# A decoder kernel whose retrieval weights are products of the keys' exponentials, taken beside the second cross attention

## The chip, the cores and the metric

The kernel runs on one core of a Trainium2 chip. The metric is device microseconds of one execution, from its start to its end; the time of a kernel is the median of several executions. A profiled execution also records every instruction of the engines TensorE (PE, with its weight loads as PEld), VectorE (DVE), ScalarE (ACT), GpSimd (POOL) and SyncE (SP), with the semaphores that they wait for.

## The reference

Two decoder layers run over 16 blocks `x` of 128 rows and 256 columns. Each has a self attention, a cross attention on 16 blocks `ctx` and a feed-forward part, and a layer normalisation behind each of the three. The change concerns the feed-forward part of the second layer. It is the sum of a gated MLP and of a retrieval over 512 experts:

```python
n = b * s                                             # 2048 rows
queries = (hidden_states @ W_q).reshape(2, n, 64)
routing = jnp.einsum('tnd,tdk->tnk', queries, keys)   # two lists of 64 key scores for every row
scores2, idx2 = jax.lax.top_k(routing, 8)
sx, sy = scores2[0], scores2[1]
ix, iy = idx2[0], idx2[1]
all_scores = (sx[:, :, None] + sy[:, None, :]).reshape(n, 64)
all_idx = (ix[:, :, None] * 64 + iy[:, None, :]).reshape(n, 64)
scores, pk = jax.lax.top_k(all_scores, 8)
indices = jnp.take_along_axis(all_idx, pk, axis=-1)
de, ue = down_embed[indices], up_embed[indices]       # tables of 512 rows: a larger index reads row 511
ew = jax.nn.silu(jnp.einsum('nh,nkh->nk', x, de)) * jax.nn.softmax(scores, axis=-1)
experts_states = jnp.einsum('nk,nkh->nh', ew, ue)
mlp = jax.nn.silu(x @ gate_w) * (x @ up_w) @ down_w
return mlp + experts_states
```

So a row has, in each of two lists, its 8 best of 64 key scores; of the 64 sums of those it takes the 8 best, and a softmax over them gives the weights. An index is 64 times the first key's index plus the second's, and all indices from 511 on read the last expert.

## The kernel before

**Layout.** All numbers are f32. `x_t[b]` is block b, 128 rows on the partitions, 256 columns. The retrieval reads the 2048 x 128 queries as two lists of 2048 x 64, so output row 2*(R*128+p)+hf takes list one from row p of block R and list two from row p of block 8+R, columns 64*hf to 64*hf+63 of the query in both. The kernel therefore works in NR = 8 groups R, each with two halves `hf` of 128 rows. The weights of one group are a tile `E` of 128 x 2 x 512: a full row of 512 experts for every row, with zeros where an expert isn't chosen. That way no table is gathered: two dense matrix products with all 512 experts do the work.

**The two attentions of the second layer** are laid out in beats by `by_beats`. A block of the cross attention has 4 units of scores, one per beat. Each unit is a product into a PSUM tile `ps_st` of 128 x 1024, whose row maximum DVE takes (`nm`); six beats later the scores are computed a second time, with the maximum subtracted, and ACT takes their exponential `pT`. The sums over values and over ones go to `ps_o`. Beside the units stand jobs, each with an offset in beats from the first unit of its block; those of one beat are issued in the order of their list, behind the beat's units:

```python
        cross_block = (
            4, 6, cross_scores(pl, 8, kept1, 6),
            [(3, cross_parts), (4, cross_maxima), (11, cross_out), (12, cross_invert), (13, cross_add), (14, cross_scale),
             (1, values), (-2, queries), (18, turn_block), (19, route), (23, lambda b: score(0, b)),
             (25, lambda b: score(1, b)), (26, best)],
            [b for R in range(NR) for b in (R, NR + R)],
        )
```

`cross_out` copies `ps_o` to `ol` on ACT; `cross_invert` turns the sums over ones into their reciprocals by a logarithm and an exponential on ACT; `cross_add` adds the residual (`xn`) on DVE and takes the statistics of the normalisation, of which POOL computes `rstd` by a power; `cross_scale` normalises into `x_t[b]` on DVE. `queries` makes the masked copies `z` on POOL. `turn_block` transposes the finished block, and ACT copies it into `fxT`, the transposed input of the last feed-forward part. `route`, `score` and `best` run only for the second block of a group (b = 8+R): `route` multiplies with W_q (`fq_T` is the copy on ACT), `score` multiplies with the keys, once per half (ACT copies into `rt`), and `best` takes on DVE the 8 best of each list (`sv`), the 64 sums of these (`al`) and the 8 best sums (`sc`). These four hold all groups at once, in a pool `early`. The small products share one PSUM bank in two halves (`ps_half`); three tiles of two banks each serve `ps_st`.

In the beats, `vec`, `act` and `pool` issue through a wrapper at L199 that keeps the program's order, so every operation of DVE, ACT and POOL there has the line L199. TensorE's order is always kept: all products go through `mm` (L240) and all transposes through `turned` (L243). In the last block the activations that go through `act` keep the program's order (L1478); the rest is placed by a scheduler that looks at what each engine has to do.

**The last block** (from L1465 on) begins with a loop over R = 0 to 8. In each round `weights(R)` computes `E[R]` on DVE and ACT, TensorE computes three items of the gated MLP (`gate_up`: two products of 128 x 512 each into two `ps_f` banks of four, SiLU of the one to `g` on ACT, their product to `gT` on DVE), and then the eight 128 x 128 transposes of `E[R-1]` into `ps_x`, which ACT copies to `eT` (L1540). Of the 32 items 24 stand in this loop and 8 later.

`weights(R)` computes for both halves: the 512 sums `S` of the first 8 keys of list one (whole, unsorted) with all 64 of list two, which are the scores of experts 0 to 511 (DVE, L1486); `top`, the negated best sum; on ACT, per half, the exponentials `w8` of the 8 best sums with their total `z`, `wl` of the 64 best pairs and `ex` of the 512 sums, all minus the best; the mask `m` of the 64 pairs that are at least as large as the eighth best (`is_ge` with `al`), less those whose first key is one of 0 to 7, times `wl`, summed to `rest`, the weight that goes to expert 511; then per half the mask `M` of the 512 sums, its count on ACT (`none`, L1529), and E = M / z * ex (L1530), with `rest` added to the last column. The counts are summed at the end; a branch (L1640) on a total above zero would handle rows with equal scores one by one, and isn't taken here. ACT uses one table for exponentials and another for SiLU and loads one when it needs it (ACT_TABLE_LOAD). Behind the branch come `down` (product with all 512 expert rows, SiLU, times `eT`), the last 8 items, `finish` and the output.

Of the kernel before, what the change touches and what calls it, by code (L numbers as in the profile page):

```python
# [9 lines left out]
F32 = mybir.dt.float32  # L10
# [8 lines left out]
P = 128  # L19
# [12 lines left out]
def kernel(ctx: ExitStack, tc: tile.TileContext, a: dict, out: bass.AP):  # L32
# [1217 lines left out]
    sv = early.tile([P, NR, 2, 2, 8], F32, name="sv")  # L1250
    al = early.tile([P, NR, 2, 8, 8], F32, name="al")
    sc = early.tile([P, NR, 2, 8], F32, name="sc")
    with ExitStack() as st:
        pl, switch = attention_tiles(st, 6)
# [170 lines left out]
        def score(hf, b):  # L1425
            R = b - NR
            if R < 0:
                return
            ps = pl["m"].tile([P, 2, 64], F32, name="ps_m")
            rows = slice(hf * 64, hf * 64 + 64)  # L1430
            for t in range(2):
                mm(ps[:, t, :], lhsT=routes[R][rows, t, :], rhs=fkeys[rows, t, :], start=True, stop=True)
            act.copy(rt[:, R, hf], ps)

        def best(b):
            R = b - NR
            if R < 0:
                return
            for hf in range(2):
                for t in range(2):  # L1440
                    vec.max(sv[:, R, hf, t, :], rt[:, R, hf, t, :])
            vec.tensor_tensor(
                al[:, R], sv[:, R, :, 0, :].unsqueeze(3).to_broadcast([P, 2, 8, 8]),
                sv[:, R, :, 1, :].unsqueeze(2).to_broadcast([P, 2, 8, 8]), ALU.add,
            )
            for hf in range(2):
                vec.max(sc[:, R, hf, :], al[:, R, hf].rearrange("p i j -> p (i j)"))

# [3 lines left out]
             (1, values), (-2, queries), (18, turn_block), (19, route), (23, lambda b: score(0, b)),  # L1452
             (25, lambda b: score(1, b)), (26, best)],
            [b for R in range(NR) for b in (R, NR + R)],
# [7 lines left out]
    with ExitStack() as st:  # L1462
# [17 lines left out]
        def weights(R):  # L1480
# [8 lines left out]
            )  # L1489
            top = hp.tile([P, 2], F32, name="top")  # L1490
            nc.vector.tensor_scalar_mul(top, sc[:, R, :, 0], -1.0)
            w8 = hp.tile([P, 2, 8], F32, name="w8")
            wl = hp.tile([P, 2, 64], F32, name="wl")
            ex = hp.tile([P, 2, 512], F32, name="ex")
            z = hp.tile([P, 2], F32, name="z")
            for hf in range(2):
                one = top[:, hf : hf + 1]
                act(w8[:, hf, :], sc[:, R, hf, :], AF.Exp, bias=one, accum_out=z[:, hf : hf + 1])
                act(wl[:, hf, :], al[:, R, hf].rearrange("p i j -> p (i j)"), AF.Exp, bias=one)
                act(ex[:, hf, :], S[:, hf].rearrange("p a b -> p (a b)"), AF.Exp, bias=one)  # L1500
            rz = hp.tile([P, 2], F32, name="rz")
            nc.vector.reciprocal(rz, z)

            si = hp.tile([P, 2, 8], U32, name="si")
            for hf in range(2):
# [5 lines left out]
            nc.vector.tensor_tensor(  # L1511
                m, al[:, R], sc[:, R, :, 7:8].unsqueeze(3).to_broadcast([P, 2, 8, 8]), ALU.is_ge
            )
# [4 lines left out]
            nc.vector.tensor_tensor(m, m, mo, ALU.subtract)  # L1518
            nc.vector.tensor_tensor(m.rearrange("p h i j -> p h (i j)"), m.rearrange("p h i j -> p h (i j)"), wl, ALU.mult)
            rest = hp.tile([P, 2], F32, name="rest")  # L1520
# [60 lines left out]
        equal = nc.values_load(n_equal[0:1, 0:1], min_val=0, max_val=P * NR * 2 * 1024)  # L1581

        def chosen_one_by_one(st):

# [58 lines left out]

        first.close()
        hp = st.enter_context(tc.tile_pool(name="ffn_b", bufs=2))
# [115 lines left out]
```

## Time and profile before

| | us |
|---|---|
| median of 3 executions | 1466.75 (1464.52 to 1467.91) |
| profiled execution | 1463.26 |
| its span, first to last instruction | 1461.5 |
| mean granted TensorE clock | 0.954 |

Busy time by stage, in us, from the profile's busy time in windows of the span:

| window | what runs | PE | DVE | ACT | POOL | clock |
|---|---|---|---|---|---|---|
| 1186 to 1212 | end of the cross attention, first `weights` | 21.85 | 14.64 | 13.18 | 1.60 | 0.81 |
| 1212 to 1240 | first rounds of the last block | 27.49 | 18.73 | 19.42 | 0.00 | 1.00 |
| 1240 to 1300 | further rounds | 54.90 | 32.25 | 43.41 | 0.00 | 1.00 |
| 1300 to 1315 | last round, counts, branch | 12.10 | 4.51 | 7.50 | 0.00 | 0.89 |
| 1315 to 1461.5 | `down`, last items, `finish` | 135.83 | 42.06 | 14.06 | 8.80 | 0.98 |

A timeline line has the start in us, the length in us, the engine, the line of the program, the operation, what it writes and reads with partitions x elements and types, how many such instructions the line stands for, and in brackets an idle time ahead of it and what ended that. A group line has the count, the busy time and the mean in ns of one. A line of the waits has the us waited in all, the count and the longest in us. L199, L240, L243 and L1478 are lines of helpers, so the tile's name tells the operations of such a line apart.

### The profile page before, as it was taken

To read this page: it belongs to the slowest core of one execution; us is meant where nothing else is said; L and a number is where in the kernel's file an instruction comes from. 1 tells how busy PE (TensorE), PEld (TensorE's weight loads), DVE (VectorE), ACT (ScalarE), POOL (GpSimd) and SP (SyncE) were. 2 spreads that over 40 slices of the span, in tenths; PEclk is the share of its full clock that TensorE was granted. 3 is DMA by queue.
4 is the path that set the end of the run, shared out by engine and by line. 5 is a ranking of instruction groups with operands and counts; after the bars stand their busy time and mean duration, and the time that the engine had idled before them with its cause. 6 is when DMAs were issued, how large, how long until landed. Compare 5 with 4: busy or idle time off the path is not lost. (4 is left out here: it accounts for less than half of the span.)

```text
span 1461.5 us, 28762 instructions
## 1 busy us (share of the span) xinstructions
PE 1332.1 (91%) x11929; PEld 850.8 (58%) x11929; DVE 818.3 (56%) x2179; ACT 598.3 (41%) x1051; POOL 292.4 (20%) x402
## 2 busy tenths in 40 slices
PE   3999889999999945999999779999999989989997
PEld 2656555555555523777788646666555544446666
DVE  6899877787878641100001158876777756533222
ACT  1454425556556621111111125553566656761010
POOL 7000243334454120000000053311222200000000
PEclk9999979999999976999999959999999999999999
DMA  9100000000000005233222011112000000000000
GB/s 309 57 2 2 2 1 2 1 2 16 16 16 16 16 31 189 84 99 103 92 90 84 28 51 31 31 33 86 2 2 2 2 2 1 0 1 15 15 8 22
DMA packets 42716, 57.01 MB, mean 39 GB/s; under 512 B 5928, under 2 KB 32568, under 8 KB 42568
## 3 DMA queue, kind: packets, MB, share of 16 engines
q1 hardware_dynamic: 34808, 37.79, 8.1%
q0 software_dynamic: 4544, 12.21, 2.6%
q10 hardware_dynamic: 3216, 4.99, 1.0%
q8 instruction: 98, 1.61, 0.5%
q14 instruction: 50, 0.41, 0.1%
HBM read 38.60 MB, written 16.38 MB: 38 GB/s over the span
## 5 line engine op out<-in xcount | busy, mean ns | idle before, releaser
L199 DVE TENSOR_REDUCE nm<-ps_st 128x4 f32<-128x1024 f32 (+1 forms) x256 | 312.6, 1221 | 116.2 <-PE ps_st L240 115.8
L199 ACT ACTIVATE pT<-ps_st 128x1024 f32<-128x1024 f32 x224 | 229.4, 1024 | 192.0 <-PE ps_st L240 190.6
L199 POOL TENSOR_TENSOR rstd<-ve,nhalf 128x1 f32<-128x1 f32 x112 | 62.6, 561 | 683.8 <-DVE ve L199 657.1
L240 PE MATMUL ps_o<-pT,v 128*32 128x256 f32 (+1 forms) x2560 | 164.6, 348 | 1.1 <-DVE oT L199 1.1
L240 PE MATMUL ps_st<-rot,z 32*128 32x256 f32 x1024 | 150.9, 415 | 2.3 <-DVE nm L199 2.3
L1135 DVE TENSOR_TENSOR ye<-ps_e,b 128x256 f32<-128x256 f32 (+6 forms) x38 | 16.1, 424 | 236.9 <-PE ps_e L1132 236.9
L240 PE MATMUL ps_st<-z,rot 32*128 32x512 f32 x512 | 134.7, 604 | 0.0
L1124 ACT ACTIVATE h<-ps_h,b 128x672 f32<-128x672 f32 (+7 forms) x64 | 46.6, 727 | 204.3 <-PE ps_h L1120 192.3
L1120 PE MATMUL ps_h<-h,w 128*128 128x336 f32 (+7 forms) x512 | 122.1, 399 | 0.0
L1120 PEld LDWEIGHTS ps_h<-h,w 128*128 128x128 f32 x512 | 97.2, 190 | 23.6
L240 PEld LDWEIGHTS ps_o<-pT,v 128*32 128x32 f32 x2560 | 54.4, 108 | 95.9 <-issue 86.0
L240 PE MATMUL ps_st<-nmT,pick 32*128 32x256 bf16 x1024 | 101.3, 276 | 2.6 <-ACT pT L199 2.5
L240 PEld LDWEIGHTS ps_st<-rot,z 32*128 32x128 f32 x1024 | 92.9, 192 | 16.6 <-issue 4.9
L199 POOL DMA_INDIRECT y<-ys,place x32 | 31.2, 976 | 283.0 <-DVE absT L1260 275.3
L240 PE MATMUL ps_o<-pT,ones 128*32 128x256 f32 x1024 | 78.7, 379 | 0.0
L240 PEld LDWEIGHTS <-pick 32*128 32x128 bf16 x1024 | 29.2, 92 | 74.6 <-issue 67.8
L240 PE MATMUL ps_st<-ctx,z 32*128 32x256 f32 x512 | 72.2, 399 | 0.0
L240 PE MATMUL ps_f<-fxT,fgw 128*128 128x512 f32 x128 | 62.2, 609 | 6.7 <-ACT g L1478 6.7
L1132 PE MATMUL ps_e<-w,h 128*128 128x256 f32 (+6 forms) x304 | 67.3, 379 | 0.0
L1120 PE MATMUL ps_h<-xeT,w 128*128 128x336 f32 (+7 forms) x256 | 65.3, 415 | 2.1 <-DVE xeT L1112 2.1
L240 PE MATMUL ps_st<-z,ctx 32*128 32x512 f32 x256 | 65.4, 589 | 0.0
L1132 PEld LDWEIGHTS ps_e<-w,h 128*128 128x128 f32 (+6 forms) x304 | 54.9, 181 | 11.0 <-issue 1.0
(311 smaller groups left out, 2348.4 us busy)
## 6 DMA issues: line engine op xcount, KB each, us to landing
w<-in_W_dram SPq DMA_DIRECT2D x16, 512.0 KB, 3.6
w<-in_W_dram SPq DMA_DIRECT2D x8, 1024.0 KB, 6.6
xs<-zero SPq DMA_DIRECT2D x42, 128.0 KB, 3.9
xe<-xs SPq DMA_DIRECT2D x32, 128.0 KB, 3.8
ys<-ye SPq DMA_DIRECT2D x32, 128.0 KB, 2.9
x<-in_x_dram SPq DMA_DIRECT2D x16, 128.0 KB, 5.9
ctx<-in_ctx_dram POOLq DMA_DIRECT2D x16, 128.0 KB, 5.5
out_dram<-x SPq DMA_DIRECT2D x16, 128.0 KB, 1.7
```

The costliest lines, as they stand in the source:

```text
L199: instruction = getattr(self.engine, name)(*args, **kw)
L240: tc.keep_in_program_order(nc.tensor.matmul(*args, **kw))
L1120: nc.tensor.matmul(ps[:, n, 0:H], lhsT=w[:, c, hc * P : (hc + 1) * P], rhs=src[:, c, n * H : (n + 1) * H], start=(c == 0), stop=(c == part ...
L1124: nc.scalar.activation(dst[:, hc, 0:cap].rearrange("p (n t) -> p n t", n=2), ps[:, :, 0:H], AF.Gelu, bias=b12[:, layer, hc : hc + 1],)
L1132: nc.tensor.matmul(ps[0:m], lhsT=h2[:, fc, c : c + m], rhs=w3[:, fc, :], start=(fc == 0), stop=(fc == 3))
L1135: nc.vector.tensor_add(ye[0:m, c // P, :], ps[0:m], b3[0:m])
```

## The change

The exponential of a sum is the product of two exponentials. The change computes exponentials of the keys themselves, each less the best key of its list, in the cross attention of the second layer, and multiplies them in the last block.

- `best(b)` no longer keeps the 64 sums `al` for every group; it also writes `least`, the three negated maxima (of the two lists and of the sums), with two DVE operations.
- A new job `exponentials(hf, b)`, 28 and 30 beats from the first unit of the block, issues five ACT exponentials per half: `e0` of the first 8 keys of list one (8 columns), `e1` of all 64 of list two, `ev` of the 8 best of each list (twice 8 columns) and `e8` of the 8 best sums, with their total `ez`. As `route`, it does so for the second block of a group only: 16 halves in all. The results stay in `early`.
- `weights(R)` loses `top` and all its activations but the count `none`. `wl` becomes a DVE product of the two rows of `ev` (128 x 128), and `ex` a product of `e0` and `e1` on POOL (128 x 1024, one operation for both halves; both operands are read repeatedly along one dimension). The sums for the mask `m` are computed again on DVE (128 x 128). The reciprocal reads `ez`.
- The pool of `weights` is closed ahead of the branch instead of behind it.

The order of TensorE's products is the same before and after. In the order after, POOL has the two products `ex` of R = 0 and 1 ahead of the `rstd` of the last block of the cross attention, and DVE has `S`, `wl` and the first half of `E` of R = 0 ahead of that block's `x`.

```diff
--- before.py
+++ after.py
@@ -1248,8 +1248,14 @@
 
     rt = early.tile([P, NR, 2, 2, 64], F32, name="rt")
     sv = early.tile([P, NR, 2, 2, 8], F32, name="sv")
-    al = early.tile([P, NR, 2, 8, 8], F32, name="al")
     sc = early.tile([P, NR, 2, 8], F32, name="sc")
+
+
+    e0 = early.tile([P, NR, 2, 8], F32, name="e0")
+    e1 = early.tile([P, NR, 2, 64], F32, name="e1")
+    ev = early.tile([P, NR, 2, 2, 8], F32, name="ev")
+    e8 = early.tile([P, NR, 2, 8], F32, name="e8")
+    ez = early.tile([P, NR, 2], F32, name="ez")
     with ExitStack() as st:
         pl, switch = attention_tiles(st, 6)
 
@@ -1439,18 +1445,36 @@
             for hf in range(2):
                 for t in range(2):
                     vec.max(sv[:, R, hf, t, :], rt[:, R, hf, t, :])
+            al = pl["w"].tile([P, 2, 8, 8], F32, name="al")
             vec.tensor_tensor(
-                al[:, R], sv[:, R, :, 0, :].unsqueeze(3).to_broadcast([P, 2, 8, 8]),
+                al, sv[:, R, :, 0, :].unsqueeze(3).to_broadcast([P, 2, 8, 8]),
                 sv[:, R, :, 1, :].unsqueeze(2).to_broadcast([P, 2, 8, 8]), ALU.add,
             )
             for hf in range(2):
-                vec.max(sc[:, R, hf, :], al[:, R, hf].rearrange("p i j -> p (i j)"))
+                vec.max(sc[:, R, hf, :], al[:, hf].rearrange("p i j -> p (i j)"))
+            least = routes[R] = pl["w"].tile([P, 3, 2], F32, name="least")
+            vec.tensor_scalar_mul(least[:, 0:2, :].rearrange("p t h -> p h t"), sv[:, R, :, :, 0], -1.0)
+            vec.tensor_scalar_mul(least[:, 2, :], sc[:, R, :, 0], -1.0)
+
+        def exponentials(hf, b):
+            R = b - NR
+            if R < 0:
+                return
+            least = routes[R]
+            act.activation(e0[:, R, hf, :], rt[:, R, hf, 0, 0:8], AF.Exp, bias=least[:, 0, hf : hf + 1])
+            act.activation(e1[:, R, hf, :], rt[:, R, hf, 1, :], AF.Exp, bias=least[:, 1, hf : hf + 1])
+            for t in range(2):
+                act.activation(ev[:, R, hf, t, :], sv[:, R, hf, t, :], AF.Exp, bias=least[:, t, hf : hf + 1])
+            act.activation(
+                e8[:, R, hf, :], sc[:, R, hf, :], AF.Exp, bias=least[:, 2, hf : hf + 1],
+                accum_out=ez[:, R, hf : hf + 1],
+            )
 
         cross_block = (
             4, 6, cross_scores(pl, 8, kept1, 6),
             [(3, cross_parts), (4, cross_maxima), (11, cross_out), (12, cross_invert), (13, cross_add), (14, cross_scale),
              (1, values), (-2, queries), (18, turn_block), (19, route), (23, lambda b: score(0, b)),
-             (25, lambda b: score(1, b)), (26, best)],
+             (25, lambda b: score(1, b)), (26, best), (28, lambda b: exponentials(0, b)), (30, lambda b: exponentials(1, b))],
             [b for R in range(NR) for b in (R, NR + R)],
         )
         ordered[0] = True
@@ -1487,19 +1511,18 @@
                 S, rt[:, R, :, 0, 0:8].unsqueeze(3).to_broadcast(all512),
                 rt[:, R, :, 1, :].unsqueeze(2).to_broadcast(all512), ALU.add,
             )
-            top = hp.tile([P, 2], F32, name="top")
-            nc.vector.tensor_scalar_mul(top, sc[:, R, :, 0], -1.0)
-            w8 = hp.tile([P, 2, 8], F32, name="w8")
-            wl = hp.tile([P, 2, 64], F32, name="wl")
+            wl = hp.tile([P, 2, 8, 8], F32, name="wl")
+            nc.vector.tensor_tensor(
+                wl, ev[:, R, :, 0, :].unsqueeze(3).to_broadcast([P, 2, 8, 8]),
+                ev[:, R, :, 1, :].unsqueeze(2).to_broadcast([P, 2, 8, 8]), ALU.mult,
+            )
             ex = hp.tile([P, 2, 512], F32, name="ex")
-            z = hp.tile([P, 2], F32, name="z")
-            for hf in range(2):
-                one = top[:, hf : hf + 1]
-                act(w8[:, hf, :], sc[:, R, hf, :], AF.Exp, bias=one, accum_out=z[:, hf : hf + 1])
-                act(wl[:, hf, :], al[:, R, hf].rearrange("p i j -> p (i j)"), AF.Exp, bias=one)
-                act(ex[:, hf, :], S[:, hf].rearrange("p a b -> p (a b)"), AF.Exp, bias=one)
+            nc.gpsimd.tensor_tensor(
+                ex.rearrange("p h (a b) -> p h a b", a=8), e0[:, R].unsqueeze(3).to_broadcast(all512),
+                e1[:, R].unsqueeze(2).to_broadcast(all512), ALU.mult,
+            )
             rz = hp.tile([P, 2], F32, name="rz")
-            nc.vector.reciprocal(rz, z)
+            nc.vector.reciprocal(rz, ez[:, R])
 
             si = hp.tile([P, 2, 8], U32, name="si")
             for hf in range(2):
@@ -1509,14 +1532,18 @@
             nc.vector.tensor_scalar(own, own, 7.5, None, ALU.is_lt)
             m = hp.tile([P, 2, 8, 8], F32, name="m64")
             nc.vector.tensor_tensor(
-                m, al[:, R], sc[:, R, :, 7:8].unsqueeze(3).to_broadcast([P, 2, 8, 8]), ALU.is_ge
+                m, sv[:, R, :, 0, :].unsqueeze(3).to_broadcast([P, 2, 8, 8]),
+                sv[:, R, :, 1, :].unsqueeze(2).to_broadcast([P, 2, 8, 8]), ALU.add,
+            )
+            nc.vector.tensor_tensor(
+                m, m, sc[:, R, :, 7:8].unsqueeze(3).to_broadcast([P, 2, 8, 8]), ALU.is_ge
             )
             mo = hp.tile([P, 2, 8, 8], F32, name="mo")
             nc.vector.tensor_tensor(mo, m, own.unsqueeze(3).to_broadcast([P, 2, 8, 8]), ALU.mult)
             nc.vector.tensor_reduce(counts[:, R, :, 0], m.rearrange("p h i j -> p h (i j)"), AX.X, ALU.add)
             nc.vector.tensor_reduce(counts[:, R, :, 1], mo.rearrange("p h i j -> p h (i j)"), AX.X, ALU.add)
             nc.vector.tensor_tensor(m, m, mo, ALU.subtract)
-            nc.vector.tensor_tensor(m.rearrange("p h i j -> p h (i j)"), m.rearrange("p h i j -> p h (i j)"), wl, ALU.mult)
+            nc.vector.tensor_tensor(m, m, wl, ALU.mult)
             rest = hp.tile([P, 2], F32, name="rest")
             nc.vector.tensor_reduce(rest, m.rearrange("p h i j -> p h (i j)"), AX.X, ALU.add)
             E = hp.tile([P, 2, 512], F32, name="E")
@@ -1579,6 +1606,8 @@
         n_equal = sp.tile([P, 1], I32, name="n_equal")
         nc.vector.tensor_copy(n_equal, ps)
         equal = nc.values_load(n_equal[0:1, 0:1], min_val=0, max_val=P * NR * 2 * 1024)
+
+        first.close()
 
         def chosen_one_by_one(st):
 
@@ -1641,7 +1670,6 @@
             with ExitStack() as st2:
                 chosen_one_by_one(st2)
 
-        first.close()
         hp = st.enter_context(tc.tile_pool(name="ffn_b", bufs=2))
 
         def down(tb):
```

## The prediction

> **What bounds the kernel now.** I read the page first, then the waits of TensorE in the last block, then the timeline, because an average over 1461.5 us says nothing of a stage of 115 us.
>
> ```profile
> span 1461.5 us, 28762 instructions
> PE 1332.1 (91%) x11929; PEld 850.8 (58%) x11929; DVE 818.3 (56%) x2179; ACT 598.3 (41%) x1051; POOL 292.4 (20%) x402
> ```
>
> TensorE is the bound of the whole; only a place where it stands still can give time back. The wait summary of TensorE from 1196 us to the branch at 1311.2 us:
>
> ```profile
> PE ps_f L240 <- ACT g L1478: 6.7, 6, 1.1
> PE ps_half L243 <- DVE x L199: 1.5, 1, 1.5
> ```
>
> Six waits of 1.1 us on the SiLU `g`, and in the tail of the cross attention one of 1.5 us on the last block's normalised rows `x`. The timeline shows one such round:
>
> ```profile
> 1261.45 0.71 ACT L1478 ACTIVATE ex<-S,top 128x512 f32<-128x512 f32 x1
> ...
> 1263.05 0.63 ACT L1529 ACTIVATE none<-M 128x512 bf16<-128x512 bf16 x1 [0.90 <-DVE M L1525]
> ...
> 1263.79 1.28 ACT L1478 ACT_TABLE_LOAD   x1
> ...
> 1265.09 1.09 ACT L1478 ACTIVATE g<-ps_f 128x512 f32<-128x512 f32 x2
> ...
> 1265.73 1.98 PE L240 MATMUL ps_f<-fxT,fgw 128*128 128x512 f32 x4 [1.12 <-ACT g L1478]
> ...
> 1269.27 1.04 PE L243 MATMUL ps_x<-ident,E 128*128 128x128 f32 x8
> ...
> 1281.84 1.04 PE L243 MATMUL ps_x<-ident,E 128*128 128x128 f32 x8
> ```
>
> ACT does six exponentials, waits for a mask, reloads its table (1.28 us), and only then frees the PSUM bank that TensorE needs. A round lasts 1281.84 - 1269.27 = 12.57 us. What it lasts without the wait stands earlier, in the first rounds:
>
> ```profile
> 1221.28 1.88 PE L240 MATMUL ps_f<-fxT,fgw 128*128 128x512 f32 x4
> ...
> 1231.58 1.04 PE L243 MATMUL ps_x<-ident,E 128*128 128x128 f32 x8
> 1232.46 1.88 PE L240 MATMUL ps_f<-fxT,fgw 128*128 128x512 f32 x4
> ```
>
> Three items take 10.30 us and the transposes 0.88 us: 11.18 us.
>
> **The change, part by part.** The profiled execution took 1463.26 us (span 1461.5), 3.5 us under the median 1466.75 of the three runs. I sum differences against the profiled execution and put them on the median.
>
> *1. Exponentials and table loads leave the rounds.* ACT then has per round two masks (0.63 + 0.19 each), three `g` (0.60) and two `eT` (0.62): 4.7 us, no table load. Six rounds fall from 12.57 to 11.18 us: 6 x 1.39 = **-8.3 us**. What is late next? DVE is busy 32.2 us in the six slices from 1240 to 1300, so 6.8 us per round; `wl` and the rebuilt sums add 2 x 0.28 and `top` (0.16) goes: 7.2 us. If one POOL multiply stops it for its whole length (2.6 us, below) that is 9.8 of 11.18: still under TensorE. The exponentials of the last R come behind the first `g`, so one pair of table loads stays: 1.28 + 2.26 + 1.28 = 4.8 us between the first and second `g`. TensorE needs the second `g` only for its fourth item, 10.3 us after its start, and the second `g` ends near 9.3: nothing.
>
> *2. Ten small exponentials per R in the cross attention.* Rows of the same sizes: `w` (128x8) 0.30 and `wl` (128x64) 0.33 us, but they overlap: `w` and its accumulator read take 0.29 from start to start, so about 0.20 without the read; `wl` 0.24. One half (8, 64, 8, 8 columns, the last with read): 0.20 + 0.24 + 0.40 + 0.29 = 1.13 us, 16 halves. The first half of an R stands behind the pair of `ol` and ahead of a score exponential `pT`. ACT, then TensorE:
>
> ```profile
> 1116.63 0.87 ACT L199 ACTIVATE ol<-ol 128x256 f32<-128x256 f32 x2
> 1117.56 1.02 ACT L199 ACTIVATE pT<-ps_st 128x1024 f32<-128x1024 f32 x1
> ```
>
> ```profile
> 1118.83 0.48 PE L240 MATMUL ps_st<-ctx,z 32*128 32x256 f32 x2
> ```
>
> ACT has no gap there: `pT` would end near 1119.57 instead of 1118.58, and TensorE rewrites that bank at 1118.83 to 1119.15. It comes 0.4 to 0.8 us late; part returns, since the two row groups that normally share this stretch then run apart. Bounds per place 0 and 0.8; I take 0.5, the middle. Four R (0 to 3) have score tiles behind them: **+2.0 us** (0 to 3.2). The second half stands where ACT idles 0.82 us: `pT` comes 0.3 us late against a reserve of 0.8, nothing. DVE's two added `least` (0.16 each) lie ahead of a maximum whose result has about 0.5 us to spare: nothing; without that cover 8 x 0.3 = 2.4 us.
>
> *3. The tail on ACT.* The two halves of R = 6 (2.26 us) stand between `fq_T` (1206.62 to 1206.99) and the next `rt` (1208.20), where 1.2 us were idle: **+1.0 us** before TensorE reaches the first item. Those of R = 5 delay a `fkeys` product, which is over before the last `x` arrives: nothing.
>
> *4. The tail on POOL and DVE.* The sums `S` and POOL's new multiply `ex` are both released by the last `ps_o` product. POOL has two multiplies (R = 0, 1) queued ahead of the `rstd` of the last block; DVE has `wl`, a reciprocal, the rebuilt sums and one `E` (waiting for `ex`) ahead of the last `x`.
>
> ```profile
> 1197.75 1.22 DVE L1486 TENSOR_TENSOR S<-rt 128x1024 f32<-128x1024 f32 x1 [0.22 <-PE ps_o L240]
> ...
> 1202.83 0.41 DVE L199 TENSOR_SCALAR x<-xn,mv,rstd 128x256 f32<-128x256 f32 x1 [0.26 <-POOL rstd L199]
> ```
>
> ```profile
> 1202.24 0.55 POOL L199 TENSOR_TENSOR rstd<-ve,nhalf 128x1 f32<-128x1 f32 x1 [6.39 <-DVE ve L199]
> ```
>
> How long does a 128x1024 multiply take on POOL? Nearest row, one group of POOL:
>
> ```profile
> L199 POOL TENSOR_TENSOR rot<-rot,rot_t 128x256 f32<-128x256 f32 x32 | 23.2, 726 | 2.5
> ```
>
> The MEMSET rows (128x64 0.14, 128x1024 0.94 us) give 0.83 ns per column and a fixed part of 0.09. Lower bound 0.73 + 768 x 0.83 ns = 1.4 us, upper four of the slower `rot_t` rows, 3.3 us; taken 0.09 + 4 x 0.64 = 2.6 us, by the row of the same operation. Unhindered the pair ends at 1197.8 + 5.2 = 1203.0, and `rstd` starts 0.8 us late.
>
> DVE and POOL hinder each other here:
>
> ```profile
> 149.65 2.74 POOL L199 TENSOR_SCALAR z<-rot,hm 128x256 f32<-128x256 f32 x3
> ...
> 150.59 0.60 DVE L199 TENSOR_SCALAR x<-xn,mv,rstd 128x256 f32<-128x256 f32 x1
> ```
>
> This normalisation takes 0.40 us alone and 0.60 beside `z`; and `rot_t` (0.82) differs from `rot` (0.73) in that a DVE product runs when it starts. If the two exclude each other fully, about 2.1 us of each multiply stand in front of DVE (0.5 lies beside index searches), and 0.3 us of added DVE work: 2 x 2.1 + 0.3 = 4.5 us. Bounds 0.6 and 4.5; I take **+3.3 us**, nearer to the upper, because `S`, `wl`, `E` and the mask all read two tensors or a wide one from SBUF.
>
> The row first: delays of 0.2 us beside POOL operations of 0.9. [...]
>
> *5. The rest.* The pool closed ahead of the branch leaves the 1.5 us of the branch, and what follows runs in the same order on TensorE: nothing; bound one more such wait, +1.5 us.
>
> Sum: -8.3 + 2.0 + 1.0 + 3.3 = **-2.0 us**, 1464.75 us (1461.3 for an execution like the profiled one).
>
> **The rivals.**
>
> *A, the sum above*: own range -5.5 to +1.5 us (1461.25 to 1468.25), from the bounds of steps 2 and 4.
>
> *B, no exclusion*: POOL and DVE run side by side, step 4 costs 0.6: -8.3 + 2.0 + 1.0 + 0.6 = -4.7, 1462.05 us. For it: several normalisations started 0.32 us into a `z` took their usual 0.40. Against it: the 0.60 above.
>
> *C, slower: the multiply itself*. Its place is the tail, where two stand ahead of `rstd`. With full exclusion the cost is about 2X - 0.7, and above 2.6 us the first rounds, which wait for the same multiplies, stall by about twice the excess. It decides from X = 3 us; at X = 4: -8.3 + 2.0 + 1.0 + 7.3 + 2.8 = +4.8, 1471.55 us. For it: operands repeated along a dimension, which no row of POOL has. Against: the 0.73 of `rot` would have to grow more than fivefold for four times the columns.
>
> *D, slower: the cross attention*. If all ten halves of R = 0 to 4 stall TensorE for 0.8 us, step 2 costs 8 instead of 2: +4.0, 1470.75 us. Against: ACT's idle 0.82 us before every second one.
>
> **How the numbers follow.** A 0.47, B 0.25, C 0.18, D 0.10. Predicted is A. 0.2% is 2.9 us, about what a measurement of this kernel can tell from no change. Of A 0.36 lies beyond -2.9 and 0.06 beyond +2.9; of B nearly 0.9 is faster; of C and D nearly 0.9 slower. Faster 0.17 + 0.23 = 0.40; slower 0.03 + 0.24 = 0.27; within 0.33. The range, 1460.0 to 1472.0, takes in B with a cheap step 2 and C and D at their prices.
>
> **What would show it.** Step 1: no wait of TensorE on `g` in the rounds, rounds of 11.2 us, three table loads there. Step 2: TensorE waiting for `pT` about 0.5 us once per R. Step 3: `rt` 1 us later behind `fq_T`. Step 4: the length of `ex`; `S`, `M`, `xn` longer or later beside it; the wait for the last `x` grown from 1.5 to about 5 us. The prediction is wrong if TensorE still waits in the rounds (for `gT` or `E` then), or if `ex` takes over 3 us or under 1.5.

## The result and the profile after

The changed kernel takes 1460.01 us (median of 15, 1458.48 to 1464.18) against 1466.32 us for the kernel before, measured beside it (median of 15, 1462.14 to 1468.32). The ratio is 0.9967, with a 95% interval of 0.9957 to 0.9978: 4.8 us faster, 3.2 to 6.3. Two later measurements on other occasions gave 0.9988 (0.9972 to 1.0004) and 0.9991 (0.9978 to 1.0005). The forecast was -2.0 us, 1464.75 us, in a range of 1460.0 to 1472.0.

The page of the changed kernel begins with its span, then the busy time of each engine:

```profile
span 1462.5 us, 28806 instructions
PE 1333.3 (91%) x11929; PEld 853.1 (58%) x11929; DVE 837.2 (57%) x2203; ACT 580.0 (40%) x1071; POOL 311.6 (21%) x410
```

This profiled execution took 1464.18 us, the longest of its 15, while the first profile of before (1463.26 us) was one of its kernel's shorter ones. The two spans alone would say that nothing was gained. So I compared the traces place by place: TensorE's products come in the same order in both, and the difference of the start times of the same product tells how far one execution has fallen behind the other. Where that lag changes, time is lost or won. The places are the cross attention (1040 to 1190 us of before), the tail (1190 to 1237), the rounds (to 1309) and the branch (to 1325):

| against the first profile of before, us | cross attention | tail | rounds | branch | sum |
|---|---|---|---|---|---|
| changed kernel | +2.52 | +4.25 | -8.35 | -1.81 | -3.4 |
| changed_again | +2.49 | +5.61 | -8.35 | -1.85 | -2.1 |
| changed_third | +2.49 | +4.40 | -8.35 | -1.83 | -3.3 |
| before_again | 0.00 | +0.07 | +0.01 | +0.07 | +0.1 |

Ahead of 1040 us the lag is between -3.9 and +4.3 us, in code that is the same in all of them, so the whole of one execution says little; behind 1325 us it does not change by 0.01 us. The mean times of the three measurements of the changed kernel lie 4.8, 1.7 and 2.0 us below those of the kernel before.

The rounds first. The timeline of the changed kernel, all engines, one round:

```profile
1265.02 1.04 PE L243 MATMUL ps_x<-ident,E 128*128 128x128 f32 x8
...
1268.27 1.22 DVE L1510 TENSOR_TENSOR S<-rt 128x1024 f32<-128x1024 f32 x1
1268.29 0.58 ACT L1502 ACTIVATE g<-ps_f 128x512 f32<-128x512 f32 x1
1268.53 2.72 POOL L1520 TENSOR_TENSOR ex<-e,e 128x1024 f32<-128x1024 f32 x1 [8.46 <-ACT none L1556]
...
1269.41 1.86 DVE L1558 SCALAR_TENSOR_TENSOR E<-rest,rz,E 128x1 f32<-128x1 f32 x1
...
1276.19 1.04 PE L243 MATMUL ps_x<-ident,E 128*128 128x128 f32 x8
```

From transposes to transposes it is 1276.19 - 1265.02 = 11.17 us, with no table load and no wait of TensorE. DVE is held up there (an `E` of one column takes 1.86 us, 0.22 us elsewhere), and it costs nothing. The waits of TensorE from 1190 to 1318 us show where time is lost instead:

```profile
PE ps_half L243 <- DVE x L199: 3.2, 1, 3.2
PE ps_half L240 <- ACT fxT L199: 2.1, 2, 1.7
PE ps_half L240 <- ACT rt L199: 1.8, 2, 1.2
PE ps_f L240 <- PEq L1669: 1.4, 1, 1.4
```

The six waits on `g` are gone; the wait for the last `x` has grown from 1.5 to 3.2 us, and those for `fxT` and `rt` from 1.0 and 0.7 to 2.1 and 1.8. The last two stood in the kernel before, over the same window, as

```profile
PE ps_half L240 <- ACT fxT L199: 1.0, 2, 0.6
PE ps_half L240 <- ACT rt L199: 0.7, 2, 0.4
```

### The profile page after: what moved, and what is told of

Same layout as the page of the kernel before. It is cut to its first block, busy times and chain, and to the rows that moved or that the text cites. A ratio compares the mean times of both kernels' runs of the same rounds, so it can differ in the third digit from the quotient of the medians.

```text
span 1462.5 us, 28806 instructions
## 1 busy us (share of the span) xinstructions
PE 1333.3 (91%) x11929; PEld 853.1 (58%) x11929; DVE 837.2 (57%) x2203; ACT 580.0 (40%) x1071; POOL 311.6 (21%) x410
## 5 line engine op out<-in xcount | busy, mean ns | idle before, releaser
L199 ACT ACTIVATE pT<-ps_st 128x1024 f32<-128x1024 f32 x224 | 229.3, 1024 | 184.6 <-PE ps_st L240 183.7
```

Source lines behind the costliest of these rows:

```text
L199: instruction = getattr(self.engine, name)(*args, **kw)
```

## The experiments

### The added part alone, and its place on ACT

**exps_only** adds to the kernel before what the change adds in the cross attention, and leaves `weights` as it was:

```diff
+            least = routes[R] = pl["w"].tile([P, 3, 2], F32, name="least")
+            vec.tensor_scalar_mul(least[:, 0:2, :].rearrange("p t h -> p h t"), sv[:, R, :, :, 0], -1.0)
+            vec.tensor_scalar_mul(least[:, 2, :], sc[:, R, :, 0], -1.0)
...
+        def exponentials(hf, b):
...
-             (25, lambda b: score(1, b)), (26, best)],
+             (25, lambda b: score(1, b)), (26, best), (28, lambda b: exponentials(0, b)), (30, lambda b: exponentials(1, b))],
```

> The kernel before, with the 16 halves of small exponentials and the negated maxima added in the cross attention (their results are written and not read; they share two sets of buffers), and the pool closed ahead of the branch; the weights of the last block stay as before. So it is the added part of the change alone. Theory (the added half that stands behind the pair of `ol` delays one score exponential per group): in the trace TensorE falls behind the kernel before by 0.6 us at each of the groups R = 0 to 3, 2.5 us in all, then by about 1 us in the tail between `fq_T` and `rt`; the rounds of the last block stay at 12.57 us with their waits on `g`. Timed: +3.5 us, 1470 us, ratio 1.0024. Rival (ACT has room, the exponentials are free): 0 to 1 us, ratio 1.000 to 1.0007. Rival D (every half stalls TensorE): +8 us or more, ratio over 1.005.

Measured: 1466.76 us, ratio 1.0030 (1.0017 to 1.0043). The places: cross attention +2.51, tail +3.04, rounds -0.02, branch +0.03. The lag grows by 0.63 us at each of four groups and by nothing between them, as the theory has it; that the exponentials are free, and that every half stalls, are both ruled out. The tail lost three times what was expected. TensorE's waits from 1190 to 1318 us in this kernel:

```profile
PE ps_f L240 <- ACT g L1500: 7.0, 7, 1.1
PE ps_half L240 <- ACT fxT L199: 2.1, 2, 1.7
PE ps_half L240 <- ACT rt L199: 1.8, 2, 1.2
```

The exponentials of R = 5 delay the copy `fxT`, and TensorE waits 1.7 us for it instead of 0.6. In the changed kernel a later `x` hides that; here `x` is not late, and it counts. `fxT` and `rt` together move the lag by 1.09 - 0.38 + 0.86 = 1.6 us. The rest, 1.5 us, comes behind them: about 0.9 us where TensorE's clock is still at half when it is full in the kernel before (13.65 us of half clock in this tail instead of 10.24), and 0.6 us at a seventh wait on `g`.

**beats_29_30** is the changed kernel with one number changed:

```diff
-(28, lambda b: exponentials(0, b)), (30, lambda b: exponentials(1, b))
+(29, lambda b: exponentials(0, b)), (30, lambda b: exponentials(1, b))
```

> The changed kernel with the first half of the exponentials one beat later, beat 29 instead of 28: there it stands behind the copy `v` (0.37 us) ahead of an idle 0.82 us of ACT, no longer behind the pair of `ol` (0.87 us). Theory (place, not amount): the stall of 0.63 us per group goes to 0 to 0.3, so the kernel gains 1.3 to 2.5 us on the changed kernel, about 1458 us; the tail and the rounds stay as they are. Rival (the amount of work on ACT sets the delay): the stalls stay, 1460 us as the changed kernel.

Measured: 1457.68 us, ratio 0.9974 (0.9959 to 0.9989). The cross attention costs 0.01 us instead of 2.5. ACT's timeline in the changed kernel, at one of the four groups:

```profile
1098.76 0.87 ACT L199 ACTIVATE ol<-ol 128x256 f32<-128x256 f32 x2
1099.54 0.53 ACT L199 ACTIVATE e<-rt,least 128x8 f32<-128x8 f32 x2
...
1100.63 1.00 ACT L199 ACTIVATE pT<-ps_st 128x1024 f32<-128x1024 f32 x1
```

and in this one:

```profile
1097.36 1.02 ACT L199 ACTIVATE pT<-ps_st 128x1024 f32<-128x1024 f32 x1
1098.72 0.37 ACT L199 COPY v<-ps_half 128x256 f32<-128x256 f32 x1 [0.33 <-PE ps_half L243]
1098.98 0.54 ACT L199 ACTIVATE e<-rt,least 128x8 f32<-128x8 f32 x2
...
1100.09 1.00 ACT L199 ACTIVATE pT<-ps_st 128x1024 f32<-128x1024 f32 x1
```

The same 1.1 us of exponentials stands behind `ol` in the first (0.87 us, with no idle time) and behind `v` in the second, where ACT had been idle. The place sets the stall, not the amount. The tail did not stay as it was, as had been expected: in this execution it cost 5.03 us, more than in two of the three profiles of the changed kernel, and the sum of places is lower by 1.8 to 3.1 us (-5.2 against -2.1 to -3.4).

### What the rounds waited for

**no_exp_table** is the kernel before with SiLU in the place of the exponential in the six activations of `weights`. It leaves the exponential out, so its weights are other numbers, and it stands here for its time alone:

```diff
-                act(w8[:, hf, :], sc[:, R, hf, :], AF.Exp, bias=one, accum_out=z[:, hf : hf + 1])
-                act(wl[:, hf, :], al[:, R, hf].rearrange("p i j -> p (i j)"), AF.Exp, bias=one)
-                act(ex[:, hf, :], S[:, hf].rearrange("p a b -> p (a b)"), AF.Exp, bias=one)
+                act(w8[:, hf, :], sc[:, R, hf, :], AF.Silu, bias=one, accum_out=z[:, hf : hf + 1])
+                act(wl[:, hf, :], al[:, R, hf].rearrange("p i j -> p (i j)"), AF.Silu, bias=one)
+                act(ex[:, hf, :], S[:, hf].rearrange("p a b -> p (a b)"), AF.Silu, bias=one)
```

> The kernel before, with the six exponentials of each round replaced by SiLU of the same tiles and shapes (so the exponential is left out and the weights are other numbers); ACT does as much work, but needs no other table in the rounds. Theory (the two table loads of 1.28 us are what makes ACT late): with 2.6 us of loads gone and the 2.3 us of small work kept, ACT is ready in time, the six waits on `g` go, rounds last 11.2 us instead of 12.57, about -8.3 us, ratio 0.9943. Rival (it is the exponentials that keep `g` waiting): the waits stay at half, rounds near 12, -3 us or less. If the theory holds, taking the exponentials out of the rounds was not needed for the gain, only the change of tables had to go.

Measured: 1454.91 us, ratio 0.9946 (0.9924 to 0.9969). The places: cross attention 0.00, tail +1.21, rounds -8.35, the very number of the changed kernel, and branch -1.85. Its timeline, all engines:

```profile
1252.01 1.04 PE L243 MATMUL ps_x<-ident,E 128*128 128x128 f32 x8
...
1254.18 0.71 ACT L1478 ACTIVATE ex<-S,top 128x512 f32<-128x512 f32 x1
...
1255.31 0.71 ACT L1478 ACTIVATE ex<-S,top 128x512 f32<-128x512 f32 x1
...
1263.18 1.04 PE L243 MATMUL ps_x<-ident,E 128*128 128x128 f32 x8
```

Both `ex` are still there, 0.71 us each, and the round is 11.17 us, with no table load. So taking away the two table loads per round, 2.56 us, is enough to end the stall; activations of the size of the exponentials fit. That taking away the exponentials and keeping the loads would have been enough too isn't excluded: they are 2.26 us per round, and the stall was 1.39.

### POOL and DVE in the tail

Three kernels differ from the changed one in the product `ex` alone. **pool_in_order** wraps it, so that POOL keeps the program's order; **product_twice** issues it twice; **product_on_dve** gives it to DVE:

```diff
-            nc.gpsimd.tensor_tensor(
+            tc.keep_in_program_order(nc.gpsimd.tensor_tensor(
```

```diff
+            nc.gpsimd.tensor_tensor(
+                ex.rearrange("p h (a b) -> p h a b", a=8), e0[:, R].unsqueeze(3).to_broadcast(all512),
+                e1[:, R].unsqueeze(2).to_broadcast(all512), ALU.mult,
+            )
```

```diff
-            nc.gpsimd.tensor_tensor(
+            nc.vector.tensor_tensor(
```

> The changed kernel with POOL kept in the program's order: all eight products `ex` come behind the last `rstd` of the cross attention. Nothing else is edited. Theory (POOL's products of R = 0 and 1 stop DVE, and hold up `rstd`, ahead of the last `x`): TensorE's wait for the last `x` falls from 3.2 us to about 1.5 to 2, the tail gains 1.2 to 2 us, and the first rounds lose nothing, since `E` of R = 0 is needed only about 20 us later; about 1458.5 us. Rival (DVE's own added work is what delays `x`): the wait stays at 3.2 us and the time at 1460.

> The changed kernel with every product `ex` on POOL issued twice in a row (the same values once more into the same tile), so each group has 3.8 us of POOL in place of 1.9. Theory (POOL and DVE products with two operands from SBUF exclude each other for their whole length): two more products ahead of the last `rstd` delay the last `x` by 2 x 1.9 us, the wait grows from 3.2 to about 7 us; in the rounds DVE has 7.2 + 3.8 = 11.0 us of 11.2, so they hold or grow by up to 0.5 us each; +4 to +7 us on the changed kernel. Rival (no exclusion, only `rstd` queued behind POOL): also +3.8 us for the last `x`, but DVE's products keep their 0.28 us beside POOL and the rounds stay at 11.18 with room.

> The changed kernel with the product `ex` on DVE (128x1024, as `S`, which takes 1.22 us) and none on POOL. Theory (a POOL product stops DVE's two-operand work for its 1.9 us, so it takes nothing off DVE): `x` comes no later than in the changed kernel, the wait 3.2 us falls to 2.5 to 3.2; the rounds hold 11.18 us, since DVE has 7.2 + 1.2 = 8.4 us in each; 0 to -1.5 us on the changed kernel. Rival B (POOL runs beside DVE): DVE is burdened by 1.2 us more per product, the wait for `x` grows by 1 to 2 us, +1 to +2 us.

First what the changed kernel itself shows. POOL's timeline there:

```profile
1204.76 4.71 POOL L1520 TENSOR_TENSOR ex<-e,e 128x1024 f32<-128x1024 f32 x2 [2.09 <-PE ps_o L240]
1212.16 0.55 POOL L199 TENSOR_TENSOR rstd<-ve,nhalf 128x1 f32<-128x1 f32 x1 [2.69 <-DVE ve L199]
...
1224.87 1.90 POOL L1520 TENSOR_TENSOR ex<-e,e 128x1024 f32<-128x1024 f32 x1 [5.82 <-DVE E L1557]
```

and DVE's beside it:

```profile
1204.58 1.23 DVE L1510 TENSOR_TENSOR S<-rt 128x1024 f32<-128x1024 f32 x1
1205.72 1.99 DVE L1515 TENSOR_TENSOR wl<-ev 128x128 f32<-128x128 f32 x1
1207.63 0.15 DVE L1525 RECIPROCAL rz<-ez 128x2 f32<-128x2 f32 x1
...
1207.96 0.22 DVE L1529 FIND_INDEX8 si<-sv,rt 128x8 uint32<-128x64 f32 x1
1208.09 1.53 DVE L1534 TENSOR_TENSOR m<-sv 128x128 f32<-128x128 f32 x1
...
1224.90 2.95 DVE L1510 TENSOR_TENSOR S<-rt 128x1024 f32<-128x1024 f32 x1
```

A product takes POOL 1.90 us when nothing is in its way (1224.87). The pair at 1204.76 takes 4.71, since `S` is running and the first has to wait 0.9 us for its end; then `wl` (0.28 us elsewhere) stands for 1.99 us until the first is through, and `m` (0.28) for 1.53 until the second is. At 1224.87 POOL is 0.03 us ahead of `S`, and `S`, 1.22 us elsewhere, takes 2.95. The reciprocal and the index searches pass at their usual 0.15 and 0.22 us. So in these rows `ex` and an operation of DVE shut each other out for a whole instruction, whichever starts first, and only some operations of DVE are free of it. It isn't so beside every POOL operation: as the prediction noted, a normalisation that starts 0.32 to 0.35 us into a masked copy `z` (0.98 to 1.00 us there) takes its usual 0.40 us, eleven times in the kernel before. What sets `z` apart from `ex` no run here shows.

With full exclusion and its product of 2.6 us the prediction's formula for the tail gives 4.5 us, and its sum would have been -0.8; the product is 1.90 us here, and with 1.90 the same formula gives 3.1 and the sum -2.2.

**pool_in_order**: 1458.78 us, ratio 0.9976 (0.9959 to 0.9993). The wait for `x` falls from 3.2 to 1.6 us, the tail costs 3.36 us instead of 4.25 to 5.61, the rounds stay at -8.35. The theory holds, and its gain is cut short by the same exclusion. POOL in this kernel:

```profile
1205.20 0.66 POOL L199 TENSOR_TENSOR rstd<-ve,nhalf 128x1 f32<-128x1 f32 x1 [6.60 <-DVE ve L199]
1205.84 3.80 POOL L1520 TENSOR_TENSOR ex<-e,e 128x1024 f32<-128x1024 f32 x2
```

DVE in this kernel:

```profile
1205.90 1.98 DVE L199 TENSOR_SCALAR x<-xn,mv,rstd 128x256 f32<-128x256 f32 x1 [0.44 <-POOL rstd L199]
```

`rstd` sets off both: POOL starts the next product 0.06 us ahead of `x`, and `x`, 0.41 us elsewhere, takes 1.98.

**product_twice**: 1466.67 us, ratio 1.0026 (1.0009 to 1.0044), +5.0 us on the 1461.66 of the changed kernel in the same set of runs. Its waits of TensorE:

```profile
PE ps_half L243 <- DVE x L199: 6.8, 1, 6.8
PE ps_f L240 <- DVE gT L1584: 2.2, 1, 2.2
```

and two operations of DVE that stand between the four products:

```profile
1209.49 1.87 DVE L1535 CAST own<-si 128x16 f32<-128x16 uint32 x1
1211.27 2.19 DVE L1556 TENSOR_SCALAR M<-S,sc 128x512 bf16<-128x512 f32 x1
```

The wait for `x` is the 3.2 + 2 x 1.9 = 7.0 that was expected, nearly, and a stall of 2.2 us in the first rounds comes with it: rival C as the prediction had it, met only at twice the work. The places are +12.1 in the tail, with a second stretch of half clock of 3.4 us behind that stall, and still -8.35 in the rounds: two products per round fit into DVE's 11.2 us. A cast of 16 columns (0.16 us elsewhere) and a compare with one tensor (0.48) wait as well, so reading one tensor alone does not by itself set a DVE operation free.

**product_on_dve**: 1455.06 us, ratio 0.9952 (0.9933 to 0.9971). TensorE's waits:

```profile
PE ps_half L240 <- ACT fxT L199: 2.1, 2, 1.7
PE ps_half L240 <- ACT rt L199: 1.8, 2, 1.2
PE ps_f L240 <- PEq L1669: 1.4, 1, 1.4
```

None for the last `x`, which went further than the theory, and the tail costs 2.57 us. The rounds hold. On DVE the product takes 1.22 us; on POOL it took 1.90 us of POOL and as much of DVE. A part of the gain may be order: the scheduler now puts the last block's `xn` right behind the first product, and no run separates the two. The second measurement:

> The changed kernel with the product on DVE, again, beside the changed kernel on one chip. Its first profile had no wait for the last `x` any more, and 0.9952 in time. Theory (the wait for `x` of about 3 us was POOL's doing; the later wait for `fxT` of 1.1 us stays): 2 to 3 us below the changed kernel, ratio to the kernel before 0.9955 to 0.9975. Rival: as the changed kernel, within 1 us.

gave 1462.03 us, ratio 0.9978 (0.9961 to 0.9995), just outside what was expected, with the changed kernel at 1463.65 in the same set of runs. The places come again (+2.51, +2.62, -8.35, -1.85, sum -5.1; in the first +2.49, +2.57, -8.35, -1.84), so the trace is more constant than the time. By the mean times it is 1.6 us below the changed kernel in this set of runs and 5.3 in the other; by the places 1.7 to 3.0.

### Put together

> Both edits of the changed kernel together: exponentials at beats 29 and 30, and POOL in the program's order. Theory: the two gains lie in different places and add up, 1.3 to 2.5 and 1.2 to 2 us, so about 1456.5 us, 3 to 4 us below the changed kernel, ratio to the kernel before about 0.9935. Rival: no gain beyond 1 us.

**combined** (beats 29 and 30, and POOL in order): 1458.19 us, ratio 0.9982 (0.9968 to 0.9995), no better than either edit alone: a miss. Cross attention +0.01 and the wait for `x` 1.3 us, as expected; but the tail cost 4.30 us where POOL in order alone had 3.36, and the branch -0.12 instead of -1.85. TensorE's clock stood at half for 17.06 us of this tail (13.66 with POOL in order alone), which costs 0.94 us in the first items (1.06 us for a product that takes 0.59 there), and again behind the branch. These two took the gain back. Its windows (columns: window, its length, PE busy and products, PEclk, DMA share, GB/s):

```profile
1196.00:1200.00 4.00, 1.58 (x7) 0.78 0.00 0
...
1208.00:1212.00 4.00, 3.58 (x7) 0.50 0.00 0
1212.00:1216.00 4.00, 4.00 (x7) 0.59 0.00 0
```

> The product on DVE, and the exponentials placed by group: R = 0 to 4 and 7 at beats 29 and 30, R = 5 and 6 at offsets that put them behind the last `rt` of group 6 and of group 7, where ACT idles. Theory (each stall of the change has its place): no 0.63 us per group, TensorE's waits for `fxT` and `rt` in the tail back to 0.6 and 0.4 us, so 4 to 5 us below the kernel with only the product on DVE; the rounds at 11.18 us. In sum the loss of the change is gone and its gain of 8.3 us stays: 7 to 9 us below the kernel before, ratio 0.994 to 0.9955. Rival: the first `g` comes late behind 4.5 us of exponentials and takes back 2 us or more.

**placed** is product_on_dve with the exponentials of every group where ACT idles:

```diff
-(28, lambda b: exponentials(0, b)), (30, lambda b: exponentials(1, b))
+(lambda i: {11: 33, 13: 34}.get(i, 29), lambda b: exponentials(0, b)),
+             (lambda i: {11: 33, 13: 34}.get(i, 30), lambda b: exponentials(1, b))
```

Measured: 1456.72 us, ratio 0.9960 (0.9947 to 0.9972), beside the changed kernel's 0.9991 in the same set of runs. Of the kernels that compute the reference's weights it is the fastest by the places: cross attention 0.00, tail +2.19, rounds -8.35, branch -1.85, sum -8.0; by the mean times 6.8 us below the kernel before, a little short of the 7 to 9 that were expected. TensorE's waits:

```profile
PE ps_half L243 <- DVE x L199: 1.9, 1, 1.9
PE ps_half L240 <- ACT fxT L199: 1.4, 2, 0.8
PE ps_half L240 <- ACT rt L199: 0.7, 2, 0.4
```

`rt` is back at the 0.7 of before, and the first `g` behind 4.5 us of exponentials brings no wait. The wait for `fxT` came down to 0.8 us, not to the 0.6 of before. With TensorE sooner at the last `x`, that wait is back at 1.9 us.

### What is chance

> The changed kernel as it is, a second profiled execution and more times, on the chip of the other runs of this call. What the change does by itself should come again at the same places and sizes, against the kernel before: +0.63 us at each of the groups R = 0 to 3, the wait for the last `x` at 3.2 us, the rounds -8.3 us. What is chance should not: the stretch of half clock near 1031 us (+1.5 us in the first profile of the changed kernel) and the missing one behind the branch (-1.4 us). Time 4 to 6 us below the kernel before, ratio 0.9955 to 0.998. Rival: these two stretches belong to the change and come again.

> The changed kernel once more, on the chip of the other runs of this call. The two measurements so far, ratios 0.9967 and 0.9988, lie on two sides of what the places add up to: +2.5 in the cross attention, +3.3 to +5 in the tail, -8.35 in the rounds, so -0.9 to -2.6 us, or 0.9982 to 0.9994, and 1.4 us less where the kernel before had a stretch of half clock behind the branch. Theory (sum of places plus chance): a ratio of 0.997 to 0.999. Rival (a gain beyond these places): 0.996 or below again.

> The kernel before as it is, a second profiled execution. What belongs to the kernel comes again: rounds of 12.57 us with six or seven waits on `g`, 1.5 us for the last `x`, 1.5 us at the branch. Theory (the half clock behind the branch and a part of the differences between executions are chance): against the first profile TensorE's products run ahead or behind by some us in steps of about 0.7 to 1.5 us at stretches of half clock that lie elsewhere, and no place of the change moves. Rival (waits on `g` in the rounds bring about the half clock behind the branch): the stretch behind the branch comes again.

**changed_again** gave 1461.66 us, ratio 0.9988 (0.9972 to 1.0004), **changed_third** 1463.65 us, ratio 0.9991 (0.9978 to 1.0005), **before_again** 1467.65 us, one run. The first is above the ratio that was expected and the second just above. The places of the change repeat to 0.03 us in the cross attention and the rounds. The tail doesn't: 4.25, 5.61 and 4.40 us.

What differs is TensorE's clock. The record of the granted clock in the traces has it at 1.00 or at 0.50 and nothing between, and in all fourteen traces the times at which it changes lie on a grid with a step of 3.41 us, which stands otherwise against the kernel in every execution. A stretch of half clock lasts one or several steps, unless the end of the record cuts it short (8.98 us in the first profile of before). Every profile has one in the tail: 10.24 us in the two of the kernel before, 13.65 in the changed kernel and changed_third, 17.07 in changed_again, whose tail is the longest. The lags ahead of 1040 us are such steps too: before_again has three stretches more than the first profile, at about 1.4 us each.

I had expected the half clock behind the branch to be chance. The kernel before again has it; the windows here are steps of that grid, with the same columns:

```profile
1312.21:1315.62 3.41, 1.57 (x13) 1.00 0.00 0
1315.62:1319.03 3.41, 3.41 (x5) 0.50 0.03 10
```

In the changed kernel the wait at the branch, from 1312.33 to 1313.70 us, is shorter and falls at the start of a step instead of its end, and the clock stays:

```profile
1312.25:1315.66 3.41, 2.03 (x6) 1.00 0.03 7
1315.66:1319.07 3.41, 3.41 (x9) 1.00 0.01 2
```

From the first to the ninth product behind the branch it is 5.21 us at half clock and 3.51 at full, a difference of 1.70 us, out of the 1.85. All three profiles of kernels that wait on `g` in their rounds (before, before_again, exps_only) have the 5.21, and of the eleven that don't wait there only combined has it (5.16). The grid tells what these four have in common. In the step ahead of the stretch TensorE was busy for 1.64, 1.57, 1.77 and 1.80 us of 3.41. In the other ten profiles the least busy step around the branch has 1.82 us (changed_again) or more, up to 2.4. So the waits on `g` have no direct part in it that these traces show. Two things differ: how long TensorE stands still at the branch (1.50 to 1.57 us in the three, 1.34 to 1.42 in the eleven), and where that falls on the grid. The rounds are 8.35 us shorter, which is no whole number of steps: the first product behind the branch comes 98.5 to 98.9 us (28.9 steps) behind the end of the tail's half clock in the three, and 88.8 to 90.2 us (26.0 to 26.4 steps) in all but one of the eleven. Combined (1.80) and changed_again (1.82) lie on two sides of a narrow border, so another change of a microsecond could take this gain away; no run was made to test that.

The stretch near 1031 us (+1.5 us) came in the changed kernel, product_twice, changed_third, placed and before_again, and not in the others: it belongs to neither kernel. The same holds there: TensorE was busy for 1.57 to 1.82 us in the step ahead of it in the five, and for 1.98 or more in the least busy step of the other nine.

## Why the prediction was right

The direction was right and the time, 1460.01, is at the low end of the range, 1460.0; that it is inside, by 0.01 us, is luck. It is 1.2 us below the range that the prediction gave its own sum A (and -5.5 to +1.5 us is not what the bounds of steps 2 and 4 add up to, which is -6.7 to +0.4). The measured -4.8 us is more than twice the -2.0 forecast; the two later measurements, -1.7 and -2.0, are near it, but their intervals take in no change.

- **Step 1**, the rounds: forecast -8.3, measured -8.35 in every profile of the changed kernel. A round is as long as the first rounds of before had shown, and that losing the table loads is enough for it is shown by no_exp_table. The three table loads that are left stand where the step had them, around the first two `g`. DVE had 42.8 us of 60 there (8.0 per round, the time it was held up included), where the step had put 7.2 plus a hindrance of 2.6.
- **Step 2**, the cross attention: +2.5 for +2.0. Mechanism, count and place right (four groups, the first half of each; moved by one beat it is gone), the stall 0.63 us where the middle of the bounds was 0.5. It shows in the lag, at the `ps_st` products behind `pT`; the list of TensorE's waits, where the prediction looked for it, does not have it.
- **Step 3**, ACT in the tail: the last wait for `rt` moves the lag by 0.9 us for the forecast 1.0. The part costed at nothing, `fxT` of R = 5, is hidden as said, but by the late `x`: in exps_only, where `x` isn't late, 0.7 us of its 1.1 stay uncovered.
- **Step 4**, POOL and DVE: +3.2 us until the last `x`'s products (the lag went from 6.83 to 10.03) for +3.3. The two halves of the term were both wrong and cancelled: the product takes 1.90 us, not 2.6, and for `wl`, `m` and `S` the exclusion beside it is full (1.99 us instead of 0.28, 1.53 instead of 0.28, 2.95 instead of 1.22), not partial. The reason given for a value near the upper bound, that these operations read two tensors or a wide one, was an estimate that no run shows: a cast of one tensor with 16 columns stood 1.87 us. With 1.9 in the full-exclusion formula, 2 x (1.9 - 0.5) + 0.3, it is 3.1. The wait for `x` grew only to 3.2 us and not to the 5 that were to show it, because TensorE comes to it 1.3 us later itself, by its longer waits for `fxT` and the first `rt`. Rival B (no exclusion) is ruled out by `wl` at 1.99 us, and rival C's point of decision is borne out by product_twice.
- **Step 5**, the rest at nothing, is the step that failed: the branch is worth -1.85 us, of which 0.15 is the wait and 1.70 TensorE's clock behind it. The text wrote that the change "leaves the 1.5 us of the branch", which is true of the wait (1.4) and false of what follows it. It did not ask what 8.35 us less ahead of the branch does to the place of its wait on the clock's grid.
- Rival D (every half stalls) is ruled out by the lag, which is flat between the four steps.

Without the branch the places of the three profiles give -1.6, -0.3 and -1.5 us (2.52 + 4.25 - 8.35, and so on), where steps 1 to 4 had -2.0; the difference is 0.5 us of the cross attention and, in changed_again, 1.3 us in the tail, where the half clock lasts longest. With the branch they are -3.4, -2.1 and -3.3. The first measurement's -4.8 (3.2 to 6.3) goes 1.4 us beyond the largest of these, and no place explains that; the kernel before ran slower there (mean 1465.7) than beside the other two (1462.8 and 1464.0). Which of the three measurements is nearest to the truth stays open within 3 us; that the change gains something is shown by the places, of which 1.7 us at the branch hang on where its wait falls.

## What to carry to other kernels

When an engine alternates between two activation tables inside a loop that another engine paces, count the loads before the arithmetic: here taking away 2.56 us of loads per round ended the stall, with 2.3 us of activations left in place. Be slow to give POOL a product like this one to relieve DVE: it held up many of DVE's operations for as long as POOL ran, 1.9 us where DVE itself needs 1.2, and it can hold up the very operation that the next engine waits for. Compare two traces by the lag of the same product, place by place, where whole executions differ by more than the change is worth. Work that is moved into an earlier stage is priced by its place in that stage's beat; one beat later the same exponentials cost 0.0 instead of 2.5 us.

## What the runs showed of the hardware

- A product of 128x1024 with both operands repeated along a dimension (`ex`) took POOL 1.90 us, less than four times the 0.73 us that the sum `rot` of 128x256 took in the kernel before.
- The exclusion beside that product also takes in DVE operations with one tensor: a cast of 16 columns stood 1.87 us (product_twice), the normalisation of 256 columns 1.98 (pool_in_order), while index searches (0.22), maxima (0.34 us for two), reciprocals (0.15), row sums (`rest`, 0.26) and the product `gT` (0.67), one of whose operands lies in PSUM, passed at their usual lengths.
- TensorE's clock goes to exactly half (0.50 granted) for whole steps of 3.41 us. At the branch and near 1031 us it did so in nine cases, with TensorE busy for 1.57 to 1.82 us of the step before; in the other 19 cases the least busy step had 1.82 us or more, and it did not. Busy time is not the whole measure: at the start of the tail the half clock came after a step with 2.25 us as well (no_exp_table).
